# Batches 0 to 2 normalized at an attention's end, and two shared-expert pieces in front of the gates

## The chip, the cores and the metric
One core of a Trainium2 chip runs the whole program in one launch. The metric is device time in microseconds (us) of that core, from repeated runs; lower is better. Engines are named as in the profile: PE (TensorE matmuls, PEld its weight loads), DVE (VectorE), ACT (ScalarE), POOL (GpSimd), SP (SyncE, which issues the DMAs). The granted TensorE clock is given as a share of full speed.

## What is computed
Activations x of 4 batches x 1024 tokens x 128 features pass through eight residual stages, each on a layer norm of x. The change touches what lies between the last four. Cut from the reference:

```python
def _layernorm(x, axis=-1, eps=1e-05):
    m = jnp.mean(x, axis=axis, keepdims=True)
    v = jnp.var(x, axis=axis, keepdims=True)
    return (x - m) / jnp.sqrt(v + eps)
...
x = x + _L2_attn_ref(_layernorm(x), ...)   # 8 heads of 16, softmax over 1024 keys
x = x + _L2_ffn_ref(_layernorm(x), ...)
x = x + _L3_attn_ref(_layernorm(x), ...)   # 16 heads of 8, in blocks of 64 keys
x = x + _L3_ffn_ref(_layernorm(x), ...)

# L2 ffn: each token is mixed with the one before it
xr = mu_r * x + (1.0 - mu_r) * x_prev
xk = mu_k * x + (1.0 - mu_k) * x_prev
r = jax.nn.sigmoid(jnp.einsum('btc,dc->btd', xr, W_r))
k = jnp.einsum('btc,dc->btd', xk, W_k)
k_act = jnp.square(jax.nn.relu(k))
out = r * jnp.einsum('btc,dc->btd', k_act, W_v)

# L3 ffn: 8 experts in 4 groups, 2 groups kept, 2 experts per token, and a shared expert
logits = xf @ w_gate.T
scores = jax.nn.softmax(logits.astype(jnp.float32), axis=-1)
... # group scores, mask, top 2, counts
shared = jax.nn.silu(xf @ sw1.T) * (xf @ sw3.T) @ sw2.T
out = shared.at[flat_idx].add(routed_out)
```

The routed rows use a flat list of (token, choice) pairs cut into the experts' spans by the counts: the rank of every expert for every token must be known before the routed part can start.

## The kernel before, in words
x lies in SBUF with 128 tokens on the partitions: 8 tiles of 128 tokens for a batch, 32 in all. A stage reads its transpose xnT (features on the partitions, 4096 tokens along them), which the layer norm writes.

**Layer norm.** `ln_sums` (L128) takes the statistics of one batch with bn_stats on DVE; the sums can be had in advance and are kept in `self.ahead`. `ln_moments` (L105) makes of them 1/sigma (rs: a sqrt on ACT, L114, and a reciprocal on DVE, L115) and the shift nm (DVE, L125). `ln_scale` (L144) writes eight normalized rows xn per batch, the even ones on ACT (L154), the odd ones on POOL (L152), transposes four at a time on PE (tp, L158) and copies each four to xnT on ACT (L164, 128x512).

**Attention** (`attention`, L1116, for L2 and L3). Its order is written out by hand: the function runs under a manual schedule, over turns of two rounds. A unit m is a group of heads of one batch, with M units in all; unit m is scanned (scores for the maxima, L1265 and L1277) while unit m-1 is weighed (scores again L1320, exp on ACT L1325) and gathered (po, L1357). Small jobs are hung into turns by `at(turn, round, what)`. `collect` sends a unit's results with DMAs on SP's queue (oc L1380, sc L1381) to tiles that hold all heads of a batch, and hangs up the steps of that batch's `finish`. So batches 0 to 2 are finished inside the loop; their `ln_sums` are too. Batch 3's results come after the last turn, and its finish stands in what follows:

- L2: transposes of the sums tp (L1476), their reciprocal rec on DVE (L1477), transposes of the values tp2 (L1483), ob = tp2 times rec on DVE (L1485), x += ob on POOL (L1489).
- L3: tp of sc (L1593), rec (L1594, L1595), tp2 of oc (L1602), att on DVE (L1603), tp3 (L1611), oo on ACT (L1612), projection pr (L1617), x += pr on DVE (L1619); the bias goes into x on POOL (L1597).

Outside of attention, the order of each engine's instructions is the scheduler's, from the order of the code and its own estimates. Engines run their own queues in order and wait for each other by semaphores, so an instruction that waits holds up all behind it on its engine. PSUM pairs of two banks come from `pair(name)` in rotation.

**L2 ffn** (`l2_ffn`, L1501). All four `ln_moments` come first, then the scaling of batches 0 and 1, then `batch(b)` with the scaling of batch b+1 ahead of it. `batch(b)` mixes a batch in two tiles m0 and m1 (ACT L1525 shifts and scales, DVE L1526 adds), then for each half of 512 tokens: kp (L1530), ka = relu (ACT L1534), squared (POOL L1535), rp (L1539), vp (L1544), r = tanh on ACT (L1548), r times vp on DVE (L1549), x += r on POOL (L1551). After batch 2 the layer norm of batches 0 and 1 for the next stage follows, at the end that of 2 and 3. Tanh and sqrt are in different activation tables, which ACT loads by instructions (ACT_TABLE_LOAD).

**L3 ffn** (`l3_ffn`). Layer norm of four batches, then `gates` (L1009): 32 matmuls gp of 8 columns (64 passes, as fp32 goes in two, L1014) and a softmax (L1017 to L1027). On DVE follow the ranks of groups and experts (`ranks`, L1648 and L1650), one-hot choices (hot), counts (cp, L1708), and span (L1724). z (L1730, in eight pieces) is the one-hot of choice by expert's span; the loop over q transposes z (zp L1753, zT L1759), multiplies (rp L1762), weighs (ri L1766), takes silu and product (sg L1771, L1772) and accumulates ph (L1775). The shared expert's work is cut into eight pieces of 512 tokens, `shared(n)`: gp_ and up (L1664, L1666, 128x512 matmuls), silu (L1668), s (L1669), op (L1672), x += op on DVE (L1676). In before the pieces stand so: 0 behind the gates, 1 behind the group mask, 2 behind the ranks, 3 behind span, 4 behind the second piece of z, and 5, 6 and 7 in the loop over q. A short tail (L1780 to L1790) adds the routed rows, and x goes out by DMA.

Of the kernel before, what the change touches and what calls it, by code (L numbers as in the profile page):

```python
# [9 lines left out]
F32 = mybir.dt.float32  # L10
AF = mybir.ActivationFunctionType
ALU = mybir.AluOpType
# [3 lines left out]
P = 128  # L16
NB, SEQ, D = 4, 1024, 128
TPB = SEQ // P
# [9 lines left out]
class Net:  # L28


    def __init__(self, ctx, tc, w, out):
        self.tc, self.nc, self.w, self.out = tc, tc.nc, w, out
        nc = self.nc
        self.ctx = ctx
        self.const = ctx.enter_context(tc.tile_pool(name="const", bufs=1))
        self.x = self.const.tile([P, NT, D], F32, tag="x", name="x")
        self.xnT = self.const.tile([P, NB * SEQ], F32, tag="xnT", name="xnT")
        self.ident = self.const.tile([P, P], F32, tag="ident", name="ident")
        make_identity(nc, self.ident)
        self.ones = self.const.tile([P, P], F32, tag="ones", name="ones")  # L40
        nc.vector.memset(self.ones, 1.0)
        self.eps = self.const.tile([P, 1], F32, tag="eps", name="eps")
        nc.vector.memset(self.eps, EPS)
        self.sums = self.const.tile([P, 2, NB, TPB], F32, tag="sums", name="sums")
        self.ahead = {}
        xv = w["L0_attn_x"].rearrange("b (i p) d -> p (b i) d", p=P)
        for b in range(NB):
            nc.sync.dma_start(self.x[:, b * TPB : (b + 1) * TPB, :], xv[:, b * TPB : (b + 1) * TPB, :])
# [45 lines left out]
    def layernorm(self, twice=None):  # L94


        tc = self.tc
        with tc.tile_pool(name="ln", bufs=2) as pool, tc.tile_pool(name="ln_ps", bufs=4, space=PSUM) as ps:
            for b in range(NB):
                self.ln_batch(pool, ps, b, twice)  # L100

    def ln_batch(self, pool, ps, b, twice=None):
        self.ln_scale(pool, ps, b, self.ln_moments(pool, b, twice), twice)
# [1 line left out]
    def ln_moments(self, pool, b, twice=None):  # L105
# [19 lines left out]
        nc.vector.scalar_tensor_tensor(nm, s, -0.5, rs, ALU.mult, ALU.mult)  # L125
        return rs, nm

    def ln_sums(self, pool, b):  # L128

        nc = self.nc  # L130

        st = pool.tile([P, TPB, 6], F32, tag="st", name="st")
        for i in range(TPB):
            nc.vector.bn_stats(st[:, i, :], self.x[:, b * TPB + i, :])
        d = pool.tile([P, TPB], F32, tag="d", name="d")
        s, q = self.sums[:, 0, b, :], self.sums[:, 1, b, :]
# [3 lines left out]
        nc.vector.tensor_add(q, q, d)  # L140
        nc.vector.tensor_add(s, st[:, :, 1], st[:, :, 4])
        self.ahead[b] = s, q

    def ln_scale(self, pool, ps, b, by, twice=None):  # L144
        nc = self.nc
        rs, nm = by
        src = self.x[:, b * TPB : (b + 1) * TPB, :]
        xn = pool.tile([P, TPB, D], F32, tag="xn", name="xn")
        for i in range(TPB):
            sl, bl = rs[:, i : i + 1], nm[:, i : i + 1]  # L150
            if i % 2:
                nc.gpsimd.tensor_scalar(xn[:, i, :], src[:, i, :], sl, bl, ALU.mult, ALU.add)  # L152
            else:
                nc.scalar.activation(xn[:, i, :], src[:, i, :], AF.Identity, bias=bl, scale=sl)  # L154
        for n in range(TPB // 4):
            tp = ps.tile([P, 4, P], F32, tag="tp", name="tp")
            for i in range(4):
                nc.tensor.transpose(tp[:, i, :], xn[:, 4 * n + i, :], self.ident)  # L158
            dst = self.tok(b * TPB + 4 * n, 512)
            src_ = tp.rearrange("p a b -> p (a b)")  # L160
            if twice is not None:
                nc.scalar.activation(dst, src_, AF.Identity, bias=twice[1], scale=twice[0])
            else:
                nc.scalar.copy(dst, src_)  # L164
# [951 lines left out]
    def attention(self, H, HD, scale, weights, prepare, finish, last=False):  # L1116
# [13 lines left out]
        nc, tc = self.nc, self.tc  # L1130
        G = H // 4
        W = 32 * H
        M = NB * G
        TURNS = 2 * TPB
        NBM = 9 if last else 2
        wq, wk, wv = weights
        with ExitStack() as c:
            one = c.enter_context(tc.tile_pool(name="at1", bufs=1))
            two = c.enter_context(tc.tile_pool(name="at2", bufs=2))
# [229 lines left out]
            def at(turn, rnd, what, *args):  # L1369
                jobs.setdefault((turn, rnd), []).append((what, args))  # L1370
# [16 lines left out]
            for b in range(NB):  # L1387

                t = b * G * TURNS
# [5 lines left out]
            for m in range(M):  # L1395
                t = m * TURNS
# [12 lines left out]

            for b in range(NB - 1):  # L1410
                at(M * TURNS + 3 + 3 * b, 1, self.ln_sums, two, b)
            t = 0
            while t < (M + 1) * TURNS or jobs:
                scans, weighs = TURNS <= t < M * TURNS, TURNS <= t < (M + 1) * TURNS
# [86 lines left out]
    def l2_ffn(self):  # L1501


        nc, tc = self.nc, self.tc
        wr, wk, wv, mr, mk = self.f2
        with ExitStack() as c_:
            ln = c_.enter_context(tc.tile_pool(name="f2l", bufs=2))
# [11 lines left out]
            def batch(b):  # L1519
                xb = self.tok(b * TPB, SEQ)  # L1520
                mixed = []
                for i, mu in ((0, mr), (1, mk)):
                    m = two.tile([P, SEQ], F32, tag=f"m{i}", name=f"m{i}")
                    nc.gpsimd.memset(m[:, 0:1], 0.0)
                    nc.scalar.activation(m[:, 1:SEQ], xb[:, 0 : SEQ - 1], AF.Copy, scale=mi[:, i : i + 1])  # L1525
                    nc.vector.scalar_tensor_tensor(m, xb, mu, m, ALU.mult, ALU.add)  # L1526
                    mixed.append(m)
                for n in range(SEQ // 512):
                    kp = ps.tile([P, 512], F32, tag="kp", name="kp")
                    nc.tensor.matmul(  # L1530
                        kp, lhsT=wk, rhs=mixed[1][:, n * 512 : (n + 1) * 512], start=True, stop=True
                    )
                    ka = two.tile([P, 512], F32, tag="ka", name="ka")
                    nc.scalar.activation(ka, kp, AF.Relu)  # L1534
                    nc.gpsimd.tensor_mul(ka, ka, ka)  # L1535
                    rp = ps.tile([P, 4, D], F32, tag="rp", name="rp")
                    vp = ps.tile([P, 4, D], F32, tag="vp", name="vp")
                    for i in range(4):
                        nc.tensor.matmul(  # L1539
                            rp[:, i, :], lhsT=mixed[0][:, n * 512 + i * P : n * 512 + (i + 1) * P], rhs=wr,  # L1540
                            start=True, stop=True,
                        )
                    for i in range(4):
                        nc.tensor.matmul(  # L1544
                            vp[:, i, :], lhsT=ka[:, i * P : (i + 1) * P], rhs=wh, start=True, stop=True
                        )
                    r = two.tile([P, 4, D], F32, tag="r", name="r")
                    nc.scalar.activation(r, rp, AF.Tanh, scale=0.5)  # L1548
                    nc.vector.scalar_tensor_tensor(r, r, 1.0, vp, ALU.add, ALU.mult)  # L1549
                    xs = self.x[:, b * TPB + 4 * n : b * TPB + 4 * n + 4, :]  # L1550
                    nc.gpsimd.tensor_add(xs, xs, r)  # L1551

            by = [self.ln_moments(few, b) for b in range(NB)]
            for b in range(2):
                self.ln_scale(ln, lps, b, by[b])
            batch(0)
            for b in range(1, NB):
                if b + 1 < NB:
                    self.ln_scale(ln, lps, b + 1, by[b + 1])
                batch(b)  # L1560
                if b == 2:
                    nx = [self.ln_moments(few, i) for i in range(2)]
                    for i in range(2):
                        self.ln_scale(ln, lps, i, nx[i])
# [88 lines left out]
    def l3_ffn(self):  # L1653
        nc, tc, f = self.nc, self.tc, self.f3
        E, HID = 8, 64
        self.layernorm()
        with ExitStack() as c:
# [18 lines left out]
                nc.vector.tensor_add(xs, op, xs)  # L1676


            score = self.gates(one, ps, f["gate"], None)
            shared(0)  # L1680
            s = one.tile([P, NT, E], F32, tag="sb", name="sb")
            nc.vector.tensor_add(s, score, f["bias"].unsqueeze(1).to_broadcast([P, NT, E]))
            pair = s.rearrange("p t (g two) -> p t g two", two=2)
# [161 lines left out]
```

## Time and profile before
| | |
|---|---|
| median of 3 runs | 2631.39 us (2629.13 to 2631.81) |
| profiled execution | 2639.67 us, its span 2638.0 us |
| mean granted TensorE clock | 0.927 |
| instructions in the span | 51055 |
| busy: PE, DVE, ACT, POOL | 2384.1, 1793.4, 1497.1, 291.6 us |
| L2 attention's last exp to the first kp or rp of L2 ffn | 1465.62 to 1484.93 us |
| first matmul of L3 attention (pp, L1205) | 1540.55 us |
| L3 attention's last exp to the first gate | 2500.80 to 2532.37 us |
| end of the span's tile (L1724), first piece of ri (L1766) | 2573.05, 2578.96 us |

Times in the table's lower half are microseconds from the start of the profiled span, as in the timeline and the chain. A row of the timeline is: start, duration, engine, line, operation, output and inputs, count; in brackets how long the engine sat idle before it and what released it. Busy PE time is measured at whatever clock was granted, so the same matmul shows twice the time at half clock. The profiled execution lies 8.3 us above the median of the timed runs; only differences between its rows are carried over.

### The profile page before, as it was taken

What the parts mean: (1) busy time and instruction counts of PE and PEld (TensorE: products, weight loads), DVE (VectorE), ACT (ScalarE), POOL (GpSimd) and SP (SyncE); (2) the same over time, 40 slices, a digit from 0 to 9 for tenths busy, and PEclk for the clock granted to TensorE, in tenths of its full rate; (3) what the DMA queues carried; (4) which work ended last, traced back from release to release, by engine and by line L of the source; (5) the groups of instructions that cost most, each with busy time, mean ns of one, the idle gap of its engine ahead of it and who ended that gap; (6) DMA issues with size and microseconds to landing.
All of it is one profiled execution on the core that took longest, in us unless ns stands there. A gap on an engine that the chain in (4) does not pass through costs nothing.

```text
span 2638.0 us, 51055 instructions
## 1 busy us (share of the span) xinstructions
PE 2384.1 (90%) x19913; PEld 1216.0 (46%) x19913; DVE 1793.4 (68%) x3670; ACT 1497.1 (57%) x3333; POOL 291.6 (11%) x525
## 2 busy tenths in 40 slices
PE   5688768899997979999999779999999999999878
PEld 4455435599996434333333443333333333333256
DVE  5889878466675767767775358767777777777343
ACT  4466458555554443666666635666666666656722
POOL 6012021000002440000000340000000000000011
PEclk8699879899998889999999879999999999999968
DMA  1333230000000000100010000000000000000000
GB/s 45 74 76 75 68 82 1 1 1 2 1 1 2 1 8 10 22 14 14 14 19 6 5 5 10 8 10 9 8 9 11 10 8 8 11 8 8 5 17 18
DMA packets 116719, 46.66 MB, mean 18 GB/s; under 512 B 88473, under 2 KB 111097, under 8 KB 116474
## 3 DMA queue, kind: packets, MB, share of 16 engines
q1 hardware_dynamic: 116474, 43.35, 8.3%
q8 instruction: 159, 2.61, 0.4%
q14 instruction: 86, 0.70, 0.1%
HBM read 17.04 MB, written 12.98 MB: 11 GB/s over the span
## 4 chain that ended last, share of the span: by engine, by line
PE 55%; DVE 4%; ACT 2%; POOL 1%; issue 1%; SPq 0%; DMA 0%; POOLq 0%; DVEq 0%; ACTq 0%
PE pb L1320 30%; PE po L1357 16%; PE pa L1265 2%; DVE bm L1277 1%; ACT es L1325 1%; PE pp L1205 1%; PE pe L1320 1%; DVE bm L1304 1%; PE pv L1186 1%; PE tp L158 1%; PE rp L1762 1%; PE gp L1014 1%; DVE bm L1308 0%; PE pr L1617 0%; PE kp L1530 0%
## 5 line engine op out<-in xcount | busy, mean ns | idle before, releaser
L1325 ACT ACTIVATE es<-pb 128x512 f32<-128x512 f32 x1462 | 795.7, 595 | 496.1 <-PE pb L1320 339.3
L1320 PE MATMUL pb<-q,k 32*128 32x512 f32 x2924 | 905.8, 640 | 3.2 <-DVE bm L1308 1.7
L1265 PE MATMUL pa<-k,q 32*128 32x512 f32 x2944 | 844.4, 648 | 10.2 <-DMA q<-q 10.2
L1277 DVE TENSOR_REDUCE bm<-pa 128x2 f32<-128x1024 f32 x496 | 604.6, 1224 | 260.5 <-PE pb L1320 168.0
L1357 PE MATMUL po<-es,v 128*32 128x256 f32 (+1 forms) x5760 | 474.8, 405 | 0.0
L1320 PEld LDWEIGHTS pb<-q,k 32*128 32x128 f32 x2924 | 295.3, 183 | 325.7 <-ACT es L1325 170.4
L1357 PEld LDWEIGHTS po<-es,v 128*32 128x32 f32 x5760 | 117.2, 108 | 528.7 <-issue 489.3
L1273 DVE TENSOR_REDUCE bm<-pa 128x16 f32<-128x1024 f32 x240 | 293.0, 1221 | 97.3 <-PE pb L1320 60.7
L1265 PEld LDWEIGHTS pa<-k,q 32*128 32x128 f32 x2944 | 233.5, 186 | 36.8 <-issue 18.5
L152 POOL TENSOR_SCALAR xn<-x,rs,nm 128x128 f32<-128x128 f32 x112 | 49.6, 459 | 1187.9 <-DVE nm L125 1013.7
L366 DVE TENSOR_TENSOR pr<-T,L 128x31 f32<-128x31 f32 (+15 forms) x248 | 91.7, 370 | 27.9 <-DMA L<-ld 20.6
L369 DVE TENSOR_TENSOR T<-T,pr 128x31 f32<-128x31 f32 (+15 forms) x248 | 93.1, 376 | 8.5
L158 PE MATMUL tp<-ident,xn 128*128 128x128 f32 x224 | 46.3, 357 | 42.5 <-ACT xn L154 38.0
L1364 DVE COPY oT<-po 128x512 f32<-128x512 f32 x48 | 32.7, 682 | 64.7 <-PE po L1357 64.7
L821 ACT ACTIVATE w<-tr,half 128x128 f32<-128x128 f32 x128 | 47.1, 368 | 48.3 <-PE tr L819 45.6
L796 ACT ACTIVATE a<-hp,wb 128x128 f32<-128x128 f32 x128 | 47.1, 368 | 41.6 <-PE hp L792 40.1
L1081 PE MATMUL ep<-L_ffn_expert_w,xnT 128*128 128x512 f32 x128 | 66.7, 653 | 3.3 <-DVE x L1090 3.0
L324 PE MATMUL wide<-bt,kt 32*128 32x128 f32 x512 | 30.4, 365 | 43.0 <-DVE mt L413 30.9
L486 PE MATMUL sp<-ux,kn 128*128 128x256 f32 x128 | 46.2, 494 | 17.8 <-ACT ux L475 17.7
L158 PEld LDWEIGHTS tp<-ident,xn 128*128 128x128 f32 x224 | 33.8, 178 | 60.4 <-ACT xn L154 46.9
L804 DVE TENSOR_TENSOR dlt<-gr,mask 128x128 f32<-128x128 f32 x96 | 28.0, 291 | 48.4 <-PE gr L802 48.1
L853 ACT COPY dr<-tr 128x128 f32<-128x128 f32 x128 | 34.1, 266 | 43.2 <-PE tr L851 41.1
(469 smaller groups left out, 3695.4 us busy)
## 6 DMA issues: line engine op xcount, KB each, us to landing
ld<-kk SPq DMA_DIRECT2D x128, 32.0 KB
L<-ld SPq DMA_DIRECT2D x8, 512.0 KB
td<-T SPq DMA_DIRECT2D x8, 512.0 KB
tb<-td SPq DMA_DIRECT2D x128, 32.0 KB
md<-nt SPq DMA_DIRECT2D x192, 2.0 KB
q<-md SPq DMA_DIRECT2D x192, 2.0 KB
x<-in_L_attn_x_dram SPq DMA_DIRECT2D x4, 512.0 KB
od<-o SPq DMA_DIRECT2D x32, 64.0 KB
```

Of the source, the lines that this page charges most:

```text
L152: nc.gpsimd.tensor_scalar(xn[:, i, :], src[:, i, :], sl, bl, ALU.mult, ALU.add)
L158: nc.tensor.transpose(tp[:, i, :], xn[:, 4 * n + i, :], self.ident)
L366: nc.vector.tensor_mul(pv, T[:, 0 : j + 1, j : j + 1].to_broadcast(sh), L[:, j : j + 1, j + 1 :].to_broadcast(sh))
L369: nc.vector.tensor_sub(T[:, 0 : j + 1, j + 1 :], T[:, 0 : j + 1, j + 1 :], pv)
L796: nc.scalar.activation(self.a, self.hp, AF.Silu, bias=B1)
L1081: nc.tensor.matmul(ep.rearrange("p a b -> p (a b)"), lhsT=self.tok(t), rhs=ew[:, 4 * h : 4 * h + 4, :].rearrange("p a b -> p (a b)"), star ...
L1265: nc.tensor.matmul(pa[:, j % 2, :], lhsT=st["q"][r, i * P : (i + 1) * P], rhs=st["k"][r, n * 512 : (n + 1) * 512], start=True, stop=True,)
L1273: nc.vector.tensor_reduce(out[:, :, 1:9], pa.rearrange("p j (c s) -> p j c s", c=8), axis=AX.X, op=ALU.max)
L1277: nc.vector.tensor_reduce(out[:, :, n : n + 1], pa, axis=AX.X, op=ALU.max)
L1320: nc.tensor.matmul(pb, lhsT=st["k"][r, kc * P : (kc + 1) * P], rhs=st["q"][r, n * 512 : (n + 1) * 512], start=True, stop=True,)
L1325: nc.scalar.activation(es[turn][:, j, :], pb, AF.Exp, scale=scale)
L1357: nc.tensor.matmul(po[r, cols], lhsT=vring[b % 2][:, kc, 4 * g + j, :], rhs=es[:, j, cols], start=kc == 0, stop=True, skip_group_check=True,)
```

## The change
In an attention, batches 0 to 2 are now normalized for the next stage by jobs behind the last turn of the loop: `ln_roots` takes one sqrt, reciprocal and nm for the three, `scaled(b)` writes a batch's rows into one of the tiles that exp used (es), `flipped(b)` transposes eight of them into a PSUM pair and copies 128x1024 to xnT at once. `ends` is the first turn behind the loop: roots at ends+1, rows at ends+2, +3, +4, flips at ends+3, +4, +6. The stages behind find these batches in `self.done` and normalize batch 3 alone; L2's ffn does so after queueing batch(0). In L3's ffn `shared(0)` and `shared(1)` stand in front of the gates, pieces 2, 3 and 4 each one place ahead of where the piece before them stood, and none in the loop over z.

```diff
     def layernorm(self, twice=None):
...
             for b in range(NB):
-                self.ln_batch(pool, ps, b, twice)
+                if b not in self.done:
+                    self.ln_batch(pool, ps, b, twice)
+        self.done = set()
...
+    def ln_roots(self, pool, bs):
+        nc = self.nc
+        for b in bs:
+            if b not in self.ahead:
+                self.ln_sums(pool, b)
+        for b in bs:
+            del self.ahead[b]
+        rs, nm = (pool.tile([P, len(bs), TPB], F32, tag=f"{t}{len(bs)}", name=t) for t in ("rs", "nm"))
+        own = slice(bs[0], bs[-1] + 1)
+        nc.scalar.activation(rs, self.sums[:, 1, own, :], AF.Sqrt, bias=self.eps, scale=1.0 / D)
+        nc.vector.reciprocal(rs, rs)
+        nc.vector.scalar_tensor_tensor(nm, self.sums[:, 0, own, :], -0.5, rs, ALU.mult, ALU.mult)
+        return [(rs[:, i, :], nm[:, i, :]) for i in range(len(bs))]
...
             for b in range(NB - 1):
                 at(M * TURNS + 3 + 3 * b, 1, self.ln_sums, two, b)
+
+            ends = (M + 1) * TURNS
+            by, rows = [], {}
+
+            def roots():
+                by.extend(self.ln_roots(two, range(NB - 1)))
+
+            def scaled(b):
+                t = two.tile([P, 4, 512], F32, tag="es", name="es", bufs=5)
+                rows[b] = t[:, 0:2, :].rearrange("p j (i d) -> p (j i) d", d=D)
+                self.ln_rows(rows[b], b, by[b])
+
+            def flipped(b):
+                tp = pair("lt")
+                for i in range(TPB):
+                    nc.tensor.transpose(tp[:, i * P : i * P + P], rows[b][:, i, :], self.ident)
+                nc.scalar.copy(self.tok(b * TPB, SEQ), tp)
+
+            at(ends + 1, 0, roots)
+            for b in range(NB - 1):
+                at(ends + 2 + b, 0, scaled, b)
+                at(ends + 3 + b + b // 2, 1, flipped, b)
+            self.done = set(range(NB - 1))
...
-            by = [self.ln_moments(few, b) for b in range(NB)]
-            for b in range(2):
-                self.ln_scale(ln, lps, b, by[b])
+            by = self.ln_moments(few, NB - 1)
+            self.done = set()
             batch(0)
+            self.ln_scale(ln, lps, NB - 1, by)
             for b in range(1, NB):
-                if b + 1 < NB:
-                    self.ln_scale(ln, lps, b + 1, by[b + 1])
                 batch(b)
...
+            shared(0)
+            shared(1)
             score = self.gates(one, ps, f["gate"], None)
-            shared(0)
...
-            shared(1)
+            shared(2)
             rank = self.ranks(one, s, E)
-            shared(2)
+            shared(3)
...
-            shared(3)
+            shared(4)
...
-                if q == 8:
-                    shared(4)
```

`ln_rows` is the part of `ln_scale` that writes the rows, now a function of its own.

More of the change, by code (lines that the diff above doesn't have):

```diff
@@ L142, in ln_sums, with ln_rows @@
         self.ahead[b] = s, q
-    def ln_scale(self, pool, ps, b, by, twice=None):
+    def ln_rows(self, xn, b, by):
         nc = self.nc
@@ L147, in ln_scale @@
         src = self.x[:, b * TPB : (b + 1) * TPB, :]
-        xn = pool.tile([P, TPB, D], F32, tag="xn", name="xn")
         for i in range(TPB):
@@ L154, in ln_scale @@
                 nc.scalar.activation(xn[:, i, :], src[:, i, :], AF.Identity, bias=bl, scale=sl)
+    def ln_scale(self, pool, ps, b, by, twice=None):
+        nc = self.nc
+        xn = pool.tile([P, TPB, D], F32, tag="xn", name="xn")
+        self.ln_rows(xn, b, by)
         for n in range(TPB // 4):
@@ L1551, in batch @@
                     nc.gpsimd.tensor_add(xs, xs, r)
-            by = [self.ln_moments(few, b) for b in range(NB)]
-            for b in range(2):
-                self.ln_scale(ln, lps, b, by[b])
+            by = self.ln_moments(few, NB - 1)
+            self.done = set()
             batch(0)
+            self.ln_scale(ln, lps, NB - 1, by)
             for b in range(1, NB):
-                if b + 1 < NB:
-                    self.ln_scale(ln, lps, b + 1, by[b + 1])
                 batch(b)
```

## Prediction
> **What bounds the kernel now.** I read the page's chain first, to see which engine sets the time; then the chain and the waits inside the stretches that the change touches (an attention's end and the stage behind it); then the timeline for durations, and busy time by stretch for the TensorE clock. The page, then the chain after the L2 attention's last exp (start, duration, what):
> ```profile
> PE 55%; DVE 4%; ACT 2%; POOL 1%; issue 1%; SPq 0%; DMA 0%; POOLq 0%; DVEq 0%; ACTq 0%
> ...
> 1471.83 1.88 DMA sc<-oT
> 1473.76 1.04 PE tp L1476 x8
> 1474.80 1.92 PE tp L1483 x8
> 1476.74 1.24 DVE ob L1485
> 1478.12 3.79 PE tp L158 x16
> 1482.51 1.05 ACT m L1525
> 1483.59 1.29 DVE m L1526
> 1484.93 1.22 PE rp L1539 x4
> ```
> The 55% are the attention loops, which stay. At their ends engines wait for each other: batch 3's sums return by DMA, its finish (tp, ob) stands on PE in front of the transposes of batches 0 and 1, and only then are these mixed (m) and does the ffn start, at 1484.93. The end of that stage, from the timeline:
> ```profile
> 1521.67 2.19 ACT L1525 ACTIVATE m<-xnT,mi 128x1023 f32<-128x1023 f32 x2
> 1530.47 2.16 PE L1544 MATMUL vp<-wh,ka 128*128 128x128 f32 x16 [0.51 <-POOL ka L1535]
> 1532.51 2.49 POOL L1551 TENSOR_TENSOR x<-x,r 128x512 f32<-128x512 f32 x2 [1.10 <-DVE r L1549]
> 1536.59 0.30 ACT L114 ACTIVATE rs<-sums,eps 128x8 f32<-128x8 f32 x1 [1.11 <-DVE sums L140]
> ```
> Batch 3's mix comes last and everything after it is a chain to the next stage. The L3 attention's end, from the timeline, then three stretches of it (PE, PEld, DVE, ACT and POOL busy, granted clock, DMA):
> ```profile
> 2509.21 1.00 PE L1593 MATMUL tp<-ident,sc 16*128 16x16 f32 x8 [7.31 <-DMA sc<-oT]
> 2520.31 1.22 DVE L1619 TENSOR_TENSOR x<-pr,x 128x1024 f32<-128x1024 f32 x1 [6.94 <-PE pr L1617]
> 2521.59 3.64 PE L158 MATMUL tp<-ident,xn 128*128 128x128 f32 x16 [1.32 <-DVE x L1619]
> 2532.37 13.83 PE L1014 MATMUL gp<-L_ffn_w_gateT,xnT 128*128 128x8 f32 x64 [0.67 <-ACT xnT L164]
> 2546.05 2.05 PE L1664 MATMUL gp__26630<-xnT,L_ffn_sw1T 128*128 128x512 f32 x2
> 2548.18 1.28 ACT L1668 ACT_TABLE_LOAD   x1 [15.87 <-PE gp__26630 L1664]
> ...
> 2521.60:2525.00 3.40, 3.40 (x16) 3.26 (x16) 2.20 (x13) 1.73 (x3) 1.28 (x3) 0.50 0.00 0
> 2539.00:2545.00 6.00, 6.00 (x30) 6.00 (x30) 0.00 (x0) 0.00 (x0) 0.00 (x0) 0.50 0.00 0
> 2546.00:2574.00 28.00, 20.69 (x79) 13.47 (x79) 22.29 (x64) 7.14 (x9) 0.00 (x0) 0.74 0.12 36
> ```
> Batches 0 to 2 could be normalized while PE waits 7.31 us for the sums; instead they come after x of batch 3. The 64 gate passes take 13.83 us at half clock although PE shows full; in the routing arithmetic behind them DVE (22.29 of 28) binds, not PE.
>
> **The change part by part.** The order of instructions on each engine comes from the changed program, the durations from rows of before. [...]
>
> *L2 attention's end.* One sqrt for three batches replaces three: nm comes about 0.8 earlier. The rows of batches 0 to 2 (4 of .40 on ACT, 4 of .46 on POOL each) start at 1468.15; PE flips two batches before the sums land. ACT then has copy, rows of batch 2, copy: done at 1475.05. m of batch 0 therefore starts 7.4 earlier than in before (1482.41). But the queues now hold four m's (batches 0 and 1) on ACT, 1475.05 to 1479.4, and on DVE, four of 1.29, to about 1481.3, and on DVE they stand **in front of** batch 3's reciprocal (1474.84 in before). Behind it wait tp2 (1.97: 1483.85), ob (1.23: 1485.1), and POOL's x (2.36: 1487.5, 7 later than before); and the first kp sits in PE's queue behind tp2 and waits for ob: 1485.2 against 1484.93. The start gains nothing (-0.3).
> What is gained lies behind. Batch 1 is already mixed at 1481.3 (in before ACT mixed it from 1492.59), so PE goes from batch 0 to 1 without waiting; batch 2's m's fall at about 1500 to 1504, batch 3's first at 1504.5, its second at 1517.6 (1522.7 in before), since the order still puts two batches of the next layer norm in front of it. Then kp, relu, square, vp, r and x as in the rows above, only without the 12 rp passes (2.93) that stood before kp: last x at 1529.75 against 1535.0, sums at 1531.35 against 1536.56. Gain 5.2. The walk crosses four engines, so I take 5 with ends of 8 and 0 (nothing if batch 3's second m keeps its old time).
> Against this part speaks a rule. Tanh and sqrt alternate more often: eight table loads between the first relu and the last tanh, where there were five. The rows say 1.28 each, with the activation following at once (2548.18 + 1.28, then silu at 2549.47): 3.84, while fewer copies and m's are left behind that point, so ACT's work stays about 34 us in a stretch of 45. The Trainium skill ("ScalarE: Activation LUTs", What ACT_TABLE_LOAD costs) adds a drain, 2.66 in all: then 4.1 more (3 x 1.38), on the engine that must deliver m, and the gain would be about 1. The trace shows no drain, so I keep 5.
>
> *L3 attention's end.* Here too rows start 0.9 earlier and two flips fit before the sums. The third flip waits for a copy and lies on PE between tp sc and tp oc: 2510.2 to 2512.2, so batch 3's chain (oc, att, oo, pr, x) slips by 2.0: x at 2523.6. POOL's bias add of batch 3 moves behind twelve rows, 2508.6 to 2510.9, needed at 2522: hidden by 11 us. In return ACT and PE are free at the end: sums 2525.9, sqrt, rows, two copies (4.0): xnT complete at 2529.86 against 2532.32. Gain 2.5; ends 1 and 4.
>
> *Shared pieces in front of the gates.* Four matmuls of 128x512 (two passes each) now precede the first gate, and op of both pieces (8 passes of 128x128, 1.05 warm, 1.97 cold) sit after the ninth gate. Rows: 2.05 per matmul cold, 1.02 warm. Dense matmuls lift the clock within one to two windows (it rose at 2525.0, 3.4 after 2521.59), so about 5 us cold, then warm: 6.5 us, ends 5.85 and 8.2. The gates inherit the warm clock until it falls again: the rows of before say that gates alone never lift it (0.50 for 12 us at full PE). I take three us of the 13.83 saved. Gates end 2529.9 + 6.5 + 1.05 + 10.8 = 2548.3 against 2546.05; ends 2543.7 (all gates warm, 6.9) and 2554.0 (all cold). The Trainium skill ("TensorE: Matmul & The Clock Gate", Part 1) says that about 3.4 us of activity release the throttle whatever the number of matmuls; by it the gates, entered warm, would stay warm: 2543.7, 4.6 better than mine. The trace's 0.50 decides.
> Behind the gates: silu's table is loaded already, so exp starts 4.0 after them instead of 5.3, but x of piece 2 stands before the reciprocal on DVE and waits for op: g is ready 8.15 after the gates against 7.92 (+0.2). Three to four s/x operations of .6 leave the DVE chain: -1.8. So past and span come 2.25 + 0.2 - 1.8 = 0.65 later than at 2573.05. Then piece 4 is gone from z: in before, gp and up of piece 5 and op of 4 lay cold between ri0 (2578.96) and ri2 (2588.80, 15.75 after span); now u comes after eight z's and ri0 0.5 to 1.4 later, ri2 11.6 (warm) to 14.3 (cold) after span; I take 13.0: -2.7. From there q is PE-bound with pieces 5 to 7 as before; one operation less at the tail: -0.3. Sum for the shared part: 0.65 - 2.7 - 0.3 = -2.35, which already holds xnT's 2.5. No DMA is moved, SP's queue is the same.
>
> Total: -5.0 - 2.35 = -7.4: 2631.4 - 7.4 = 2624.0.
>
> **The rivals.** (1) *The L2 gain is eaten by the queues.* For it: reciprocal behind four m's, first kp behind ob, extra table loads; against it: batch 1 is mixed when PE wants it. Then L3 alone: 2629.0, within what a measurement here can tell from no change (0.2%, 5.3 us).
> (2) *The gates inherit the warm clock throughout.* For it: dense 512-column work just ahead. Against: 0.50 in the stretch above. -5 - 2.35 - 4.6: 2619.4.
> (3) *Slower: the clock.* PE's dense stretches are broken up: the ffn of L2 starts with sparse kp and rp, and the shared pieces meet a cold PE in front of a cold row of gates. The L2 ffn had 36.2 us of PE work at clock 0.81; at 0.65 that is 45.1, 8.9 more, of which I put three quarters on the path: 6.7 - 5.0 = +1.7. L3: gates at 2554.0 (5.7 later than mine) and q started cold (ri2 at 14.3, +1.3): -2.35 + 7.0 = +4.65. Together +6.3: 2637.7. It decides with the gates cold to the last and L2's clock below some 0.67. For it: 0.50 in most of 2502 to 2546; against it: dense 6 us of matmuls, the very form that lifted the clock at 2548.96.
> (4) *It doesn't do what it says.* Rows or flips could fall inside the loop and cost PE there; in the changed order all stand after the last gather, so this is left out.
>
> **How the numbers follow.** Forecast 0.50 (own range 2620 to 2627), rival 2 0.10, rival 1 0.25, rival 3 0.15. L3's ends (-8 to +4.7) and L2's (-8 to 0) add spread: faster by over 0.2% takes most of the forecast, rival 2, a part of rival 1: 0.60; same 0.25; slower 0.15. Range 2616 to 2635: it leaves out rival 3's upper half and the best corner.
>
> **What would show it.** After the L2 attention: m of batch 0 near 1475, rec after the m's near 1481, first kp near 1485, next stage's first pp about 5 earlier than 1540.55. After L3: xnT complete 2.5 earlier relative to the last exp, gate passes partly at .108, past and span within 1 us of before, ri2 about 13 after span. Wrong if kp comes after 1488, if second m of batch 3 is not earlier, or if gates end over 5 us later than in before.

## The result and the profile after

The changed kernel takes 2627.86 us (median of 20 runs, 2622.64 to 2636.18), the kernel before 2634.01 (20 runs, 2629.13 to 2643.07): ratio 0.9975, 95% interval 0.9966 to 0.9984, so 6 to 7 us less. The profiled execution has a span of 2623.4 us, 14.6 below the profile of before. That is more than the runs show, because executions of one and the same kernel differ by several us here. Below, stretches between two events are compared, and each from more than one execution where it matters. The experiments ran in three groups on other chips, where the kernel before took 2638.9, 2635.0 and 2638.7 in the median: every ratio is against the kernel before of its own group, and medians of different groups should not be compared.

L2's end in the profile after, from the chain of waits (start, duration, what; the chain counts of a step only what lies on it, each of the four mixes m takes 1.28 on DVE):
```profile
1472.98 0.98 DVE m L1572
1474.18 0.82 DVE m L1572
1475.38 0.66 DVE m L1572
1476.57 1.28 DVE m L1572
1477.85 0.48 DVE rec L1523
1478.38 1.99 PE tp L1529 x8
1480.39 1.24 DVE ob L1531
1481.76 2.05 PE kp L1576 x2
```
The four mixes stand on DVE in front of batch 3's reciprocal, and everything down to the first kp comes behind it. The last exp ended at 1462.92, so kp starts 18.8 after it; in before the first rp came 19.3 after it. The end of that stage, from the timeline (start, duration, engine, line, operation, idle before and releaser):
```profile
1515.64 1.15 ACT L1571 ACTIVATE m<-xnT,mi 128x1023 f32<-128x1023 f32 x1
1516.81 1.28 ACT L1594 ACT_TABLE_LOAD   x1
1518.10 1.09 ACT L1594 ACTIVATE r<-rp 128x512 f32<-128x512 f32 x2
1522.95 3.78 PE L1590 MATMUL vp<-wh,ka 128*128 128x128 f32 x16 [1.00 <-POOL ka L1581]
1530.38 0.30 ACT L117 ACTIVATE rs<-sums,eps 128x8 f32<-128x8 f32 x1 [1.81 <-DVE sums L158]
```
Counted from the last exp, ACT's part of batch 3's second mix ends 53.9 after it (1516.79) instead of 58.2 (1523.86 in before), and the last sqrt starts 67.5 after it instead of 71.0. The table load follows the activation within 0.02 and the tanh follows the load within 0.01.

L3's end, from the timeline:
```profile
2505.72 0.64 PE L1638 MATMUL tp<-ident,sc 16*128 16x16 f32 x8 [2.15 <-DMA sc<-oT]
2506.29 1.50 PE L1450 MATMUL lt<-ident,es 128*128 128x128 f32 x8
2507.58 1.91 PE L1647 MATMUL tp<-ident,oc 128*128 128x128 f32 x8
2516.45 1.23 DVE L1664 TENSOR_TENSOR x<-pr,x 128x1024 f32<-128x1024 f32 x1 [5.70 <-PE pr L1662]
2524.05 2.07 PE L1709 MATMUL gp__26556<-xnT,L_ffn_sw1T 128*128 128x512 f32 x2 [0.67 <-ACT xnT L187]
2529.18 2.07 PE L1037 MATMUL gp<-L_ffn_w_gateT,xnT 128*128 128x8 f32 x18
2531.11 2.03 PE L1717 MATMUL op<-L_ffn_sw2T,s 128*128 128x128 f32 x16
2532.98 5.66 PE L1037 MATMUL gp<-L_ffn_w_gateT,xnT 128*128 128x8 f32 x46
```
PE's idle time before tp of the sums fell from 7.31 to 2.15: two flips lie in it. The third lies between tp and the value transposes. The gates are no longer one block of 13.83: 18 passes in 2.07, then the op passes, then 46 passes in 5.66. What the clock did meanwhile is in the busy time by stretch (stretch, length, PE, PEld, DVE, ACT, POOL busy, granted clock, DMA share, GB/s):
```profile
2524.00:2527.40 3.40, 3.35 (x4) 1.51 (x5) 0.00 (x0) 1.88 (x2) 2.64 (x6) 0.51 0.00 0
2531.00:2533.00 2.00, 2.00 (x20) 2.00 (x20) 0.69 (x1) 0.00 (x0) 0.00 (x0) 1.00 0.00 0
2535.00:2537.00 2.00, 2.00 (x20) 2.00 (x19) 0.00 (x0) 0.00 (x0) 0.00 (x0) 1.00 0.74 219
2537.00:2538.50 1.50, 1.50 (x12) 1.50 (x11) 0.00 (x0) 0.00 (x0) 0.00 (x0) 0.68 0.00 0
```
The clock rose at 2527.3, 3.3 after the first shared matmul, held through most of the gates and fell at 2537.5.

Where the time of the two profiles went, by stretch ("span" is the end of the tile span, L1724 before; "the end" here and below is the end of the last x on DVE, after which the output's DMA takes 2.8 more):

| stretch | before | after |
|---|---|---|
| start to L2's last exp (program unchanged) | 1465.62 | 1462.92 |
| to L3's first pp | 74.93 | 71.50 |
| to L3's last exp (program unchanged) | 960.25 | 962.84 |
| to x of batch 3 | 20.73 | 20.42 |
| to the first matmul of L3's ffn | 10.84 | 6.37 |
| to the last gate (after: shared pieces and op passes included) | 13.83 | 14.59 |
| to span | 26.85 | 25.71 |
| span to the end | 62.14 | 56.25 |

Two rows stand out. L3's attention, which the change doesn't touch, is 2.6 longer. And L3's ffn gains 6 behind span, where I had expected 3.

### The profile page after: what moved, and what is told of

It is laid out like the page before. It is cut to its first block, busy times and chain, and to the rows that moved or that the text cites. A ratio compares the mean times of both kernels' runs of the same rounds, so it can differ in the third digit from the quotient of the medians.

```text
span 2623.4 us, 51024 instructions
## 1 busy us (share of the span) xinstructions
PE 2376.9 (91%) x19913; PEld 1208.0 (46%) x19913; DVE 1794.1 (68%) x3662; ACT 1497.1 (57%) x3325; POOL 291.6 (11%) x525
## 4 chain that ended last, share of the span: by engine, by line
PE 55%; DVE 4%; ACT 2%; issue 1%; POOL 1%; SPq 0%; DMA 0%; POOLq 0%; DVEq 0%; ACTq 0%
PE pb L1343 30%; PE po L1380 16%; PE pa L1288 2%; DVE bm L1300 1%; ACT es L1348 1%; PE pp L1228 1%; PE pe L1343 1%; DVE bm L1327 1%; PE pv L1209 1%; DVE bm L1331 0%; PE rp L1806 0%; PE pr L1662 0%; PE kp L1576 0%; PE ph L1819 0%; PE vp L1590 0%
## 5 line engine op out<-in xcount | busy, mean ns | idle before, releaser
L170 POOL TENSOR_SCALAR es<-x,rs,nm 128x128 f32<-128x128 f32 x24 | 10.3, 448 | 949.2 <-DVE nm L143 948.2
L844 ACT ACTIVATE w<-tr,half 128x128 f32<-128x128 f32 x128 | 47.0, 367 | 48.4 <-PE tr L842 45.7
L181 PE MATMUL tp<-ident,xn 128*128 128x128 f32 x176 | 35.7, 348 | 38.6 <-ACT xn L172 36.8
L170 POOL TENSOR_SCALAR xn<-x,rs,nm 128x128 f32<-128x128 f32 x88 | 40.1, 469 | 234.2 <-DVE ang L600 106.2
L152 DVE BATCH_NORM_STATS2 st<-x 128x6 f32<-128x128 f32 x224 | 51.4, 279 | 11.5 <-POOL x L1597 3.8
```

## The experiments

My theory for the first four runs: each part is worth what its own stretches show. The rivals are named run by run. That L2's part is handed back in L3's attention, by the TensorE clock, became the theory only behind these four.

**Each part alone.** Only L2's end:
```diff
-            at(ends + 1, 0, roots)
-            ...
+            if not last:
+                at(ends + 1, 0, roots)
+                ...
```
(with `l3_ffn` of before).

> Only the L2 attention's end normalizes batches 0 to 2; the L3 end and the order of shared pieces are those of the kernel before. Theory (the gain of 6 us is the sum of a part at L2 and a larger part at L3): from L2's last exp to L3's first pp 71.5 us instead of 74.9, the rest unchanged, median 3 to 4 us below before. Rival (L2 gives nothing, its 3.4 us in one trace are chance): 74 to 75 us in that stretch, median equal to before.

Measured: 2632.97 us, ratio 0.9984 (0.9971 to 0.9996). Last exp of L2 to first pp 71.90, first pp to last exp of L3 962.92. The time fell by about what the theory had (0.16%, some 4 us), but not for the theory's reason: "the rest unchanged" did not hold. The sum of the two stretches is 1034.82, against 1035.18 in the profile of before. This execution is shorter in L3's end, where its code is that of before: 129.0 from L3's last exp to the end, against 134.4.

Both attention ends, with `l3_ffn` of before:

> Both attention ends normalize three batches, shared pieces stand as in the kernel before (gates first). Theory: xnT is complete about 4.8 us earlier after L3's last exp (26.8 against 31.6); the gates still take 13.8 us at half clock, so gates end near 40.6 after the last exp, and span about 4 to 5 earlier; with L2's 3.4 the median is 7 to 8 below before, and what the shared pieces add in the changed kernel is small. Rival (the gain of L3 is the warm clock on the gates): without the shared pieces in front the stretch from last exp to span is less than 3 shorter than in before, and the median only 4 to 6 below.

Measured: 2635.58 us, ratio 0.9996 (0.9982 to 1.0010). First gate 27.2 after L3's last exp, last gate 41.05, span 69.44 (before 72.25), the end 129.36. The gates ran at half clock:
```profile
2526.15 13.82 PE L1037 MATMUL gp<-L_ffn_w_gateT,xnT 128*128 128x8 f32 x64 [0.68 <-ACT xnT L187]
```
So xnT came earlier and the gates ended near 41, as the theory had it, and yet the time was that of the kernel before: theory (7 to 8 us) and rival (4 to 6) both put the gain too high. The rival's sign, a stretch to span less than 3 shorter, holds against the first profile of before (2.8) and not against its second (73.69 to span, so 4.2).

The order of the shared pieces alone (`l3_ffn` of after in the kernel before):

> Only the order of the shared pieces is changed (two in front of the gates), the layer norms stay as in the kernel before. Theory: clock rises 3.4 to 6.8 us into the four 512-column matmuls and holds for the op passes and most of the gates, so from the first shared matmul to the last gate 14 to 17 us against 13.8 for the gates alone, but ri2 comes 3 to 4 us earlier after span: median 2 to 5 below before. Rival (the gates come later and nothing is given back): span 2 us later, median equal to or above before.

Measured: 2633.17 us, ratio 0.9982 (0.9966 to 0.9998). First shared matmul to last gate 14.57, ri2 12.1 behind span, span to the end 56.26 as in the changed kernel, against 62.14; L3's last exp to the end 126.5. The theory's ranges held.

The changed kernel a second time:

> The changed kernel once more, for the stretches of a second execution. Theory: L2 stretch 71.5, L3 stretch (last exp to end) 123 to 127, median 6 us below before. Rival (the first trace was a lucky one at L3, the clock's windows falling well): L3 stretch 128 to 132.

Measured: 2631.02 us, ratio 0.9973 (0.9960 to 0.9987); stretches 71.40, 963.03 and, from L3's last exp to the end, 126.90. Between both executions of the same code lie 3.6 us at L3's end. The timeline of the second shows where: the shared matmuls ran longer at half clock.
```profile
2526.18 2.07 PE L1709 MATMUL gp__26556<-xnT,L_ffn_sw1T 128*128 128x512 f32 x2 [0.68 <-ACT xnT L187]
2528.05 1.91 PE L1711 MATMUL up<-xnT,L_ffn_sw3T 128*128 128x512 f32 x2
2529.75 1.91 PE L1709 MATMUL gp__26569<-xnT,L_ffn_sw1T 128*128 128x512 f32 x2
2531.46 1.25 PE L1711 MATMUL up<-xnT,L_ffn_sw3T 128*128 128x512 f32 x2
```
From the first of them to the first gate it took 6.37, against 5.13 in the first execution, and the 64 gate passes with the op passes took 11.42 against 9.46.

**What lengthens L3's attention.** Going through the copies of oT, one by one, the 2.6 to 2.8 us are lost before the first of them (88 us after the first pp) and stay constant to the last, 874 us later. In these first 88 us, two places differ. The projection of v, before and after, and the first weighing, before and after (timeline; on PE, DVE and ACT the two kernels issue the same instructions here):
```profile
1565.05 3.02 PE L1186 MATMUL pv<-L_attn_v_wT,xnT 128*128 128x128 f32 x16 [2.39 <-DVE bm L1277]
1594.65 0.69 PE L1320 MATMUL pb<-q,k 32*128 32x512 f32 x1 [1.05 <-DVE bm L1304]
```
```profile
1559.00 3.78 PE L1209 MATMUL pv<-L_attn_v_wT,xnT 128*128 128x128 f32 x16 [2.40 <-DVE bm L1300]
1589.67 1.22 PE L1343 MATMUL pb<-q,k 32*128 32x512 f32 x1 [0.79 <-DVE bm L1327]
```
And the clock in the 5.4 us from the first weighing on, before and then after (busy time by stretch, clock in the third column from the end):
```profile
1594.60:1600.00 5.40, 5.18 (x30) 2.94 (x30) 5.33 (x10) 2.88 (x6) 0.00 (x0) 1.00 0.00 0
```
```profile
1589.60:1595.00 5.40, 5.33 (x22) 4.14 (x24) 3.95 (x6) 2.25 (x4) 0.00 (x0) 0.50 0.00 0
```
Counted from the first pp, the weighing starts 1.15 later in after, and it runs at half clock. The clock changes only at the edges of fixed windows: all its changes in one execution, 74 to 88 of them, stand at multiples of 3.413 us from each other to within 0.01, in each of the 14 executions profiled. In before it rose at 1593.2, just ahead of the weighing; in after at 1595.5, 5.8 us into it. Measured from the window's edge, L3's first pp stood at 1.9 to 2.5 in the executions with the old L2 end and at 0.3 to 0.5 with the new one. To test whether this place sets the length, I delayed L3's start by work of no use:
```diff
             nx = [self.ln_moments(few, i) for i in range(2, NB)]
+            for _ in range(7):
+                nc.vector.tensor_scalar_mul(nx[1][1], nx[1][1], 1.0)
```

> The changed kernel with seven more DVE operations of some 0.2 us (nm times 1.0) in the chain ahead of the last layer norm of L2's ffn: L3's attention starts about 1.5 to 1.7 us later, nothing else is touched. Theory (L2's gain is returned in the first 90 us of L3's attention by the clock, since the clock's fixed windows of 3.41 us now fall badly on its head: first pp 0.4 us after a window's edge costs 2.7 us more than 1.9 after it): the stretch from first pp to last exp falls from 963.0 to near 960.3, and the last exp of L3 comes no later, rather 1 us earlier, despite the added work. Rival (the L3 attention's head is longer because of something that the earlier hand-over does on the other engines): 963.0 stays, the last exp comes 1.6 later.

Measured: 2630.15 us, ratio 0.9971 (0.9958 to 0.9984), no more than the changed kernel. Last exp of L2 to first pp 73.38 (+1.9 against 71.4 to 71.5), first pp to last exp of L3 961.18 (-1.7 to -1.9): together 1034.56, against 1034.34 and 1034.43. Nearly two us of added work in the chain cost 0.1 to 0.2. The first pp now stood 1.7 behind an edge, and the first weighing began at full clock (its row, then the clock by stretch):
```profile
1595.54 0.69 PE L1343 MATMUL pb<-q,k 32*128 32x512 f32 x1 [1.19 <-DVE bm L1327]
1595.20:1600.60 5.40, 5.06 (x26) 3.81 (x29) 4.88 (x9) 2.39 (x4) 0.00 (x0) 0.69 0.00 0
```
The rival (963.0, last exp later by the delay) is out; the theory's 960.3 was 0.9 too low, and the last exp did not come 1 us earlier as it had said.

All 14 executions, those of the kernels below included, sort the same way. In the eight whose first pp stood 0.0 to 0.5 behind an edge, L3's attention took 962.8 to 963.0, and the first weighing began 55.1 to 55.3 after the first pp at half clock, which lasted until 61.0 to 61.4. In the six where it stood 1.7 to 2.7 behind, the attention took 960.3 to 961.2, and the clock rose at 51.9 to 52.9, ahead of the first weighing (54.0 to 54.7). So the loss is some 2 us once, whatever was gained ahead of it: it eats a gain of 2 to 3 nearly whole, while of the 7.2 that the kernel with the reciprocal in front (below) gains on the old end 5.4 arrive.

The kernel before a second time:

> The kernel before once more, for the stretches of a second execution. Theory (its first profile began L3's end at a bad place of the clock's windows, 3.0 us behind an edge): last exp of L2 to last exp of L3 again 1034.6 to 1035.2, L3's end 129 to 132 instead of 134.4. Rival (the stretch is as long in every execution): 134 again.

Measured: 2635.82 us, ratio to the other runs of the same kernel 1.0002 (0.9991 to 1.0013). L2's stretch 73.68, L3's attention 960.60, sum 1034.28; L3's last exp to the end 132.78, 0.8 above what was expected, and below the rival's 134. So the 74.93 of the first profile was long by 1.3; the old L2 end takes 73.5 to 73.7.

The changed kernel without L2's part (`if last:` around the new jobs, `l2_ffn` of before):

> The changed kernel without the L2 part: L2's attention end and ffn as before, L3's end and the shared pieces as changed. Theory (L2's part is returned by the head of L3's attention): last exp of L2 to last exp of L3 1034.3 to 1035.2 as in the changed kernel (1034.4), and the median within 2 of the changed kernel's, 5 to 7 below before. Rival (L2's part is worth its 2 to 3.4 us in most executions): median 3 us or more above the changed kernel's.

Measured: 2630.19 us, ratio 0.9967 (0.9955 to 0.9980). Stretches 73.47 and 961.01, sum 1034.48. Without L2's part the kernel is as fast as with it. What L3's earlier layer norm adds to the new order of the shared pieces is not shown: without it (the order alone) L3's last exp to the end took 126.5, with it 123.3, 126.9 and here 128.8, and the ratios of the order alone (0.9982) and of this run overlap.

**The gates and the clock.** The op passes of pieces 0 and 1 behind all gates instead of behind the ninth. `shared(n, True)` (its definition is not shown) does all but op and x and returns these two as a function:

```diff
-            shared(0)
-            shared(1)
+            back = [shared(0, True), shared(1, True)]
             score = self.gates(one, ps, f["gate"], None)
+            for out in back:
+                out()
```

> The changed kernel with the op matmuls of shared pieces 0 and 1 behind all gates instead of behind the ninth. Theory (gates do not hold the clock up, the sixteen op passes among them did): the clock falls one window earlier, some 7 us after it rose and not 10, and the last 15 to 20 gate passes take 0.216 each; last gate 0 to 1.5 us later for the same work, span 0 to 1 later. Rival (once warm the gates keep the clock): all passes at 0.108, last gate 2 us earlier.

Measured: 2629.52 us, ratio 0.9979 (0.9968 to 0.9990). The last gate comes 41.16 after L3's last exp (41.38 in the first profile of after), span 66.65 (67.09). The clock, by stretch:
```profile
2533.00:2535.00 2.00, 2.00 (x20) 2.00 (x20) 0.00 (x0) 0.00 (x0) 0.00 (x0) 1.00 0.00 0
2536.20:2538.00 1.80, 1.80 (x11) 1.80 (x10) 0.00 (x0) 0.00 (x0) 0.00 (x0) 0.50 0.00 0
```
It rose between 2529.0 and 2529.6 and fell at 2536.1, some 6.8 later, where in after it had held for 10.2: one window less, and in the last window there were only gates. With gates alone the clock falls; in after, the op passes among them had held it. In time the two orders are equal, since here the op passes no longer delay the gates.

Op passes among the gates do not always hold it. The second execution of the changed kernel:
```profile
2532.55 2.07 PE L1037 MATMUL gp<-L_ffn_w_gateT,xnT 128*128 128x8 f32 x18
2534.48 2.03 PE L1717 MATMUL op<-L_ffn_sw2T,s 128*128 128x128 f32 x16
2536.34 7.63 PE L1037 MATMUL gp<-L_ffn_w_gateT,xnT 128*128 128x8 f32 x46
```
Here the clock rose at 2531.9, 5.7 after the first shared matmul, and fell at 2538.8, after 6.8. Nine profiled executions have op passes among the gates. In three of them 1.5 to 2.0 us of these passes lay in the second window behind the rise, and the clock held 10.2; in the other six it was 1.1 to 1.2, and the clock held 6.8, as with none. What counted here is how much dense work fell into a window, and the windows' place decided that: in the first profile of after the first shared matmul stood 0.2 behind an edge, in the second 1.1.

**Orders at L2's and L3's end.** The reciprocal of batch 3 ahead of all mixes, those of batch 1 behind ob:
```diff
-                    nc.vector.scalar_tensor_tensor(m, xb, mu, m, ALU.mult, ALU.add)
+                    if b < 2:
+                        with tc.issue_after((self.rec, self.ob)[b].ins):
+                            nc.vector.scalar_tensor_tensor(m, xb, mu, m, ALU.mult, ALU.add)
+                    else:
...
```
(`self.rec` and `self.ob` are the instructions that write rec and ob of batch 3; the lines that keep them are not shown.)

> The changed kernel with the order on DVE set by hand at L2's end: batch 3's reciprocal ahead of all four mixes, those of batch 1 behind ob. Theory (the four mixes in front of the reciprocal hold PE's first kp): reciprocal 5 us earlier, first kp 4 to 5 us earlier after the last exp (14 to 15 instead of 18.8), and L2's stretch 2 to 4 shorter; what of it arrives at L3's last exp depends on the clock's windows. Rival (PE is not what limits L2's ffn, batch 3's late mix is): first kp earlier, the stretch unchanged at 71.4.

Measured: 2624.54 us, ratio 0.9957 (0.9942 to 0.9972). First kp 14.2 after the last exp, L2's stretch 66.32, L3's attention 962.86, sum 1029.18: all 5.2 us arrive, since L3's attention has its long form in the changed kernel as here. The stretch lost more than the theory's 2 to 4, and the rival is out. The ratio alone does not tell this kernel from the changed one (0.9966 to 0.9984). From the timeline:
```profile
1479.80 0.56 DVE L1523 RECIPROCAL rec<-tp 128x64 f32<-128x64 f32 x1 [6.85 <-PE tp L1522]
1483.40 1.23 DVE L1531 TENSOR_TENSOR ob<-tp,rec 128x1024 f32<-128x1024 f32 x1 [0.30 <-PE tp L1529]
1484.77 2.05 PE L1580 MATMUL kp<-m,L_ffn_W_kT 128*128 128x512 f32 x2 [1.41 <-DVE ob L1531]
```
The reciprocal starts with the end of tp (1479.76) and not behind mixes. Once more:

> The kernel with the reciprocal in front of the mixes once more, for a second profile and more runs. Theory: first kp 14.2 after the last exp, L2's stretch 66 to 67, last exp to last exp 1029 to 1031, median 10 to 12 below before. Rival (the 5.2 us were one good place of the windows): last exp to last exp 1032 or more.

Measured: 2628.08 us, ratio 0.9952 (0.9934 to 0.9970); first kp 14.2, stretch 66.32, sum 1029.35. The stretches repeat to 0.2, so the rival (one good place of the windows) is out.

With this order, and batch 2's flip behind batch 3's value transposes:
```diff
-                at(ends + 3 + b + b // 2, 1, flipped, b)
+                at(ends + 3 + b + b // 2 * 3, 1, flipped, b)
```

> As the kernel with the reciprocal in front, and the flip of batch 2 behind batch 3's value transposes (in both attentions). Theory (the flip stood in batch 3's chain): x of batch 3 in L3 ready 1.0 to 1.5 earlier after the last exp (19.5 to 20.4 against 21.5), xnT complete 1 earlier. Rival (rec of batch 3 with its two DVE steps of 1.3 us is what att waits for, the flip is hidden behind it): x unchanged to 0.5 earlier.

Measured: 2616.45 us, ratio 0.9915 (0.9900 to 0.9929), 22 us below before: the fastest of all. L2's stretch 65.48, L3's attention 961.05; x of batch 3 18.0 after L3's last exp, against 21.5 with the reciprocal in front and 20.4 in the first profile of after. From its timeline:
```profile
2504.33 1.95 PE L1651 MATMUL tp<-ident,oc 128*128 128x128 f32 x8
2506.32 1.23 DVE L1652 TENSOR_TENSOR att<-tp,rec 128x1024 f32<-128x1024 f32 x1 [0.61 <-PE tp L1651]
2509.98 2.05 PE L1666 MATMUL pr<-L_attn_out_wT,oo 128*128 128x128 f32 x16 [1.14 <-ACT oo L1661]
```
att waits for tp, not for rec (done at 2505.71). It starts 10.98 after the last exp, against 12.02 and 12.13 in the two executions with the reciprocal in front: 1.0 to 1.2 from the order, as expected. A further 1.6 to 1.7 come from pr, which fell into a stretch at full clock (2.05 against 3.78 and 3.62). And the first pp stood 2.7 behind an edge, so L3's attention had its short form, 1.8 to 2.0 less. How much of this comes in every execution, one profile does not show.

Last, L2's ffn with the layer norms of batches 0 and 1 behind batch 3 (`if b == NB - 1` in place of `if b == 2`), on the kernel with the reciprocal in front:

> As the kernel with the reciprocal in front, and in L2's ffn the layer norms of batches 0 and 1 for the next stage behind batch 3 instead of ahead of it. Theory (batch 3's second mix is late since two layer norms stand in front of it on ACT): last x of batch 3 in L2's ffn 3 to 6 us earlier, but four layer norms are then left behind it (each 1.65 of rows and 1.2 of copies on ACT): L2's stretch 64 to 69, against 66.3. Rival: the layer norms do not fit in batch 3's waits, stretch 69 to 72.

Measured: 2622.84 us, ratio 0.9944 (0.9926 to 0.9961). L2's stretch 60.86, below both expectations; L3's attention 963.02, sum 1023.88, 5.3 to 5.5 less than without. The interval of the ratio overlaps that of the kernel it is built on (0.9934 to 0.9970), so the runs do not show these 5 us yet. Both last orders in one kernel were not run.

## Why the prediction was right, and where its steps were not

Forecast 2624.0 from a base of 2631.4, a gain of 7.4; the runs show 6 to 7. That the sum came out near is luck: two errors of opposite sign. Of the 5 us put on L2's part 0.4 arrived; L3's part, put at 2.35, carries the rest.

- **L2, the start (-0.3).** Right but for 0.8: rec at 1477.77, behind four mixes, first kp 0.5 earlier than the first rp in before, counted from the last exp, where 0.3 later was forecast.
- **L2, what lies behind (5, ends 8 and 0).** The mechanism was right: batch 3's second mix comes earlier and all behind it too. The size was wrong: against three executions of the old end at 73.5 to 73.7, the new end's 70.2 to 71.9 is a gain of 2 to 3. The second mix started 52.7 after the last exp, near the forecast's 52.0; the rest was lost behind it, the most by PE at half clock: vp took 3.78 for 16 passes (2.16 in before).
- **L2's gain carried to the end.** This step failed. I had written that L3's attention stays as it was and carried the 5 us through it. From last exp to last exp, four executions of the old end give 1034.3 to 1035.2 (mean 1034.6), five of the new (the changed kernel twice, L2's end alone, both ends alone, op behind the gates) 1033.0 to 1034.8 (mean 1034.2): 0.4 is left. The attention's head took the gain back, by its place in the windows of the clock; the delay and the sorting of all 14 executions show that, and the run without L2's part that nothing is missed.
- **L3's attention end (-2.5, ends 1 and 4).** The first matmul behind it came 26.8 and 27.5 after the last exp, against 30.1 to 31.6 in four executions of the old end: 3 to 5 earlier. The slip of 2.0 in batch 3's chain did not show (x 0.3 earlier in one, 0.3 to 0.4 later in the other), although the third flip lay where I had put it: with the early flips PE was at full clock until 9.4 to 9.6 after the last exp (3.8 in before), so tp took 0.64 and not 1.00, the flip 1.50 and not 1.97. But without the new order of the shared pieces this moved no time (both ends alone: ratio 0.9996), and with it no run separates what it adds.
- **Shared pieces and gates (gates end +2.25, ends -2.35 and +8).** Measured -4.0 and 0.0 in two executions (41.38 and 45.29 after the last exp, against 45.40 and 45.25 in before; the run with L2's end alone, whose gates are the old ones, had 43.9). The first of these was the lucky one: the five other profiled executions with this code at L3's end gave 45.2 to 45.7. I had saved 3 us of the gates; 6.1 were saved in one and 4.1 in the other (7.73 and 9.70 for 64 passes, against 13.83). I had left out that the op passes among the gates can renew the clock for one window. The trace's 0.50 was rightly held against the rule that the number of matmuls doesn't matter: gates alone lose the clock in every run. Rival 2, gates warm throughout (6.9 saved), was nearer in the first execution, the forecast in the second.
- **Gates to span (-1.6).** Measured 25.4 to 25.7 with the new order, 26.9 to 28.4 with the old: -1.1 to -3.1.
- **ri2 (-2.7) and the tail (-0.3).** Mis-sized, and at the wrong place. ri2 came 12.1 behind span in after, but 11.9 to 12.2 in three other executions of the old order too: the 15.75 was a PE at half clock (full clock came 10.0 behind span in that profile, 0.0 to 1.4 in the three) and no cost of piece 4. The gain lies later, where I had written that q runs as before: span to the end is 56.2 to 58.3 with the new order, 58.0 to 59.9 with the old in the three. At full clock all the way (L2's end alone 58.0, after 56.2) the last rp ends 50.7 and 48.6 behind span. PE has the same passes in both, but up to there it idles 5.1 in the old order and 4.0 in the new, where the wait of 1.07 for the first z is gone; and eight passes of ph (0.7) now stand behind the last rp, where PE waits for sg anyway. So 2 us of the 3 forecast came on the mean of these executions, for another reason than the one given.
- **Table loads.** The rule would have cost 4.1 us more by drains. The rows show none: activation, load and next activation follow each other within 0.02.
- **Rival 1** (L2's gain is lost, 2629.0) was right in its effect on L2's part, by another mechanism. **Rival 3** (slower by the clock) had the right agent, not the size: L2's ffn ran at a clock of 0.76 against 0.81, where it needed less than some 0.67.

How much of the gain comes from how often an execution hits good windows can't be settled with one or two traces per kernel: the runs of before spread over 2629 to 2647, those of the changed kernel over 2623 to 2636.

## What to carry to other kernels

Follow a gain of a few us through the next untouched stretch before counting it: compare that stretch's length too, in more than one execution. Where engines hand over, print the order of the instructions on each queue: one reciprocal of 0.55 us behind four mixes, with all that waits for it, held back some 5 us of L2's stretch, nearly what the whole change gained; with it in front and one flip moved the ratio was 0.9915, against 0.997. A narrow matmul pass took 0.11 us at full clock and 0.22 at half, so dense work that has to be done anyway can stand just ahead of such passes and among them.

## What the runs showed of the hardware

- The clock's windows of 3.413 us keep one phase for the whole execution: in the profile of before, the falls at 1470.34 and 2528.48 are 310.0 windows apart. The phase to the program's start differs from execution to execution: the first rise stood at 17.7 to 20.5 in the 14. The Trainium skill ("TensorE: Matmul & The Clock Gate", Part 1) calls the window free-running; the traces agree.
- The program falls into step with the windows: over the 14 executions profiled, L2's last exp stood 0.6 to 0.7 behind an edge in six, 2.0 to 2.1 in five, and within 0.1 of an edge in the other three, and nowhere else. What makes these three places was not tried.
- With 1.9 us of added work ahead of it, L3's attention ended only 0.1 to 0.2 later: 962.8 to 963.0 long with its first pp 0.0 to 0.5 behind a window's edge, 960.3 to 961.2 with it 1.7 to 2.7 behind.
- 64 matmul passes of 8 columns keep PE at 100% in the busy figures and neither raise the clock nor hold it: they took 13.82 to 13.83 at half clock in the four executions that ran them by themselves, and with shared matmuls ahead the clock fell after one window of gates alone. With 1.5 to 2.0 us of 128-column passes in the window it held, with 1.1 to 1.2 it fell.
